# Layer 1 of a three-layer graph network: sums by one-hot products from two-half rows, and layer 2's dense pass begun inside it

## The chip, the cores and the metric

The kernel runs on one core of one Trainium2 chip. The metric is the device time of one execution in microseconds (us). The core has five engines with an instruction queue each: TensorE (PE in the profile, its weight loads PEld), VectorE (DVE), ScalarE (ACT), GpSimd (POOL) and SyncE (SP). Each runs its own queue in order and waits for the others by semaphores. The order of the instructions is written out by hand in the program.

## The reference

Three graph convolutions on 6250 nodes with 100000 edges sorted by destination, then a residual and a layer norm.

```python
src = concatenate([edge_index[0], arange(n)]); dst = concatenate([edge_index[1], arange(n)])
deg = segment_sum(ones, dst, n);  dinv = rsqrt(deg)
norm_edge = dinv[src] * dinv[dst]
h = x                                             # 6250 x 256
for W, b in ((W1, b1), (W2, b2), (W3, b3)):       # 256x512, 512x512, 512x256
    m = h @ W
    h = relu(segment_sum(m[src] * norm_edge[:, None], dst, n) + b)
return layernorm(x + h)
```

The kernel sums the rows of h before it multiplies by W where that is narrower, and scales rows by `dinv` beforehand and afterwards. Layer 1 therefore sums rows of 256 numbers, layer 2 rows of 512, layer 3 (after W3) rows of 256.

## The kernel before, in words

The nodes are split into 50 blocks of 125 (`NB`, `Q`). A layer's rows lie in a table in HBM (`tables[0..2]`, shown as `tab`), and as two halves, a rounded float32r half and what is left, in `parts` on the chip. The sum for a block is made in one of two ways.

*Dense.* The edges into a block are counted into a matrix of 125 x 6250 bytes. `counts` makes it: it compares slots of edges with running numbers (`compared`, L1043; the running numbers `runs` lie in the upper part of the PSUM bank `near_cols`), multiplies the comparisons (L1116), copies the counts to bytes (L1078) and keeps them in HBM as `kept`. Then the bytes are converted in pieces of five (`converted`, L1349) and multiplied with `parts` in 50 products of 512 columns (L1465).

*Gathered.* POOL fetches 128 rows of the table by an indirect DMA (L1381, in `gather`). In 14 rounds, row p of a gather belongs to node p of the block, and DVE adds it to the block's `total` (L1442). What lies beyond 14 edges per node comes in three gathers per block (`beyond`), one per two blocks (`pair`) and one per ten (`shared`). These rows are split into two halves by ACT and DVE (L1434, L1437) and summed by a product with a one-hot matrix (`shot`, made at L1385; product L1397).

Which rows the rounds and the gathers beyond them fetch is found by the *finder*: `found_rounds` (L589 to L621) and `found_beyond` (L630 to L668), for two blocks at a time, 17 pairs, for the blocks from 16 on. It is a generator whose steps alternate between DVE, PE and ACT. It works in the other half of the bank `near_cols` (`spot`). A part of it runs in the set-up (before the first gather), the rest one step per gather of layer 1.

`layer(i, ...)` is the loop of a layer. One turn ("chunk") is one gather. In each turn it issues a gather, sums what was gathered a few turns ago (`SPLIT`, `ADDED`), lets every unfinished block take one step of its end (`after1`, `after2`, `after3`), lets the generators in `extras` take a step, and multiplies some dense products (at most 3 per turn in layer 1).

Layer 1: 26 blocks dense (`FEW`), 24 gathered. `after1` scales a block's sum, transposes it, multiplies it by W1 (L1516), with b1 as three bf16 rows in a product of its own (L1515), and stores the row block in `tables[1]` (L1521, L78). When all dense blocks have been summed, `caching` loads `tables[1]` back into `parts`. Layer 2: 16 blocks dense in four teams of four (`teams`: 50 units a team, each of four steps of two products, L1195; 800 steps in all), 34 gathered in rounds with rows twice as wide. When the teams are done, `home` loads the new rows of layer 3 (L1222, L1223). Layer 3: 32 blocks dense, 18 gathered.

SP issues nearly all plain loads and stores in order: table rows, `kept`, the loads of `caching` and the team's counts.

Of the kernel before, what the change touches and what calls it, by code (L numbers as in the profile page):

```python
# [10 lines left out]
F32 = mybir.dt.float32  # L11
# [27 lines left out]
SPLIT_ROWS = (5, 4, 7)  # L39
# [8 lines left out]
FEW = 26  # L48
EXTRA = 0
TEAM = 4  # L50
TEAMS = 4
PACE = (8, 11)
FRONT = 12
# [7 lines left out]
SPLIT = ((3, 4, 5), (4, 5, 6), (3, 4, 6))  # L61
ADDED = (3, 5, 3)
FIRST_EDGES = TEAM * TEAMS
G = 5
GB = Q // G

WIDE = 4
RUN = 2
HOMES = 3
# [331 lines left out]
def sorted_path(ctx: ExitStack, tc: tile.TileContext, x, edges, starts, found, wts, biases, room, late, out):  # L401
# [30 lines left out]
    tables = [dram.tile([N + 1, w], F32, name=f"tab{i}") for i, w in enumerate((C, HID, C))]  # L432
    kept = dram.tile([MANY, Q, NB * Q], U8, name="kept")
# [59 lines left out]
    at_least = finder.tile([3, 2], I32, name="eatleast")  # L493
# [4 lines left out]
    nodes_since = finder.tile([P, Q], BF16, name="esince")  # L498
    row_steps = [finder.tile([P, P], BF16, name=f"esteps{n}") for n in range(2)]
# [7 lines left out]
    spot = [mat_bank[:, :256]]  # L507
    rounds_ready, beyond_ready = set(), set()

    def finder_numbers(spare):  # L510
# [11 lines left out]
        for n in range(2):  # L522
            nc.vector.tensor_single_scalar(at_least[:, n:n + 1], part[:3], float(n + 1), op=ALU.is_ge)
# [60 lines left out]
    def found_rounds(e):  # L584
# [21 lines left out]
        run = finder.tile([Q, 2, 2 * KF], F32, name="erun")  # L606
# [18 lines left out]
    def found_beyond(e):  # L625
# [25 lines left out]
        out_of = finder.tile([P, CHOSEN, WAYS], F32, name="eout")  # L651
# [4 lines left out]
        hit = finder.tile([P, CHOSEN, KF], F32, name="ehit")  # L656
        nc.vector.tensor_tensor(hit, less.unsqueeze(1).to_broadcast([P, CHOSEN, KF]),
                                place.unsqueeze(2).to_broadcast([P, CHOSEN, KF]), op=ALU.is_equal)
        value = finder.tile([P, CHOSEN, KF], F32, name="evalue")
# [12 lines left out]
    pairs_found = [e - FIRST_EDGES for e in (*range(FEW, NB, 2), *range(FIRST_EDGES, FEW, 2))]  # L672
# [80 lines left out]
    with tc.tile_pool(name="sdeg1", bufs=1) as dp1, tc.tile_pool(name="sdeg", bufs=2) as dp, \  # L753
            tc.tile_pool(name="ps_deg", bufs=2, space=bass.MemoryType.PSUM) as psd:
        ed = dp1.tile([P, NB, KF, 2], I32, name="ed")
        dlo = dp1.tile([P, NB, KF + 1], F32, name="sdlo")
# [136 lines left out]
        with tc.manual_schedule():  # L893
# [11 lines left out]
            for table in tables:  # L905
                nc.sync.dma_start(out=table[N:N + 1, :], in_=zero[:, :table.shape[1]])
# [18 lines left out]
            for k in range(NG + 2):  # L925
                for g in (k, k - 2, k - 1):
                    if 0 <= g < NG:
                        next(stages[g])
                        if k > 0:
                            search()  # L930
                        if k > FEW // GRP + 2:
                            for _ in range(3):
                                next(finding)
                g = (FEW // GRP + k - 2) * GRP
                if k >= 2 and FIRST_EDGES // GRP * GRP <= g < NB:
                    for _ in rows_risen(g, ed, find_space):
                        pass
            for g in range(FIRST_EDGES // GRP * GRP, FEW // GRP * GRP, GRP):
                for _ in rows_risen(g, ed, find_space):
                    pass  # L940
# [24 lines left out]
    hot_rooms = [room[:, 3 * MW + n * HW:][:, :HW].bitcast(BF16)[:, :WIDE * (Q + G * NB)] for n in range(HOMES)]  # L965
    first_rows = [room[:, at:at + C] for at in range(3 * MW + HOMES * HW, room.shape[1] - 4 * C - C + 1, C)]
    b1_rows = room[:3, room.shape[1] - 3 * C:][:, :C].bitcast(BF16)
# [8 lines left out]

    shots = ctx.enter_context(tc.tile_pool(name="sshots", bufs=1))
# [10 lines left out]
    pieces = one.enter_context(tc.tile_pool(name="spieces", bufs=5))  # L988
# [7 lines left out]
    totals = totals_of(one, "sfirst_totals", C, 3)  # L996
    ps_cols = ctx.enter_context(tc.tile_pool(name="sps_cols", bufs=1, space=bass.MemoryType.PSUM))
    near = ps_cols.tile([P, 512], F32, name="near_cols")
    runs_room = room[:, room.shape[1] - 4 * C:][:, :G * NB]
    nc.vector.tensor_copy(runs_room.bitcast(BF16).rearrange("p (v w) -> p v w", w=RUN), keys.unsqueeze(2).to_broadcast([P, G * NB, RUN]))  # L1000
    nc.vector.tensor_copy(near[:, :G * NB], runs_room)
    runs = near[:, :G * NB].bitcast(BF16).rearrange("p (v w) -> p v w", w=RUN)
    bias_left = work.tile([Q, HID], F32, name="szs")[:3]
    nc.sync.dma_start(out=bias_left, in_=bass.AP(tensor=b1.tensor, offset=b1.offset, ap=[[0, 3], [1, HID]]))
# [4 lines left out]
    tr_bank = ps_sum.tile([P, HID], F32, name="str")  # L1009
    common += accs + [mm_bank, tr_bank, mat_bank]  # L1010
    spot[0] = near[:, 256:]
    for n in range(3):
        whole_rows = work.tile([Q, HID], F32, name="st")[:3, :HID // 2].bitcast(BF16)
        nc.vector.tensor_copy(whole_rows, bias_left)
        nc.vector.tensor_sub(bias_left, bias_left, whole_rows)
        if n == 0:
            nc.vector.tensor_copy(b1_rows, whole_rows)
        else:
            nc.vector.copy_predicated(b1_rows, at_least[:, n - 1:n].to_broadcast([3, HID]), whole_rows)
# [4 lines left out]
    def counts(blocks, places, rush=0, at_once=False):  # L1024
# [16 lines left out]
        def compared(out, numbers):  # L1041
            shape = list(out.shape)
            nc.vector.tensor_tensor(out, runs[:, :shape[2], :shape[3]].unsqueeze(1).to_broadcast(shape),  # L1043
                                    numbers.rearrange("p (s w) -> p s w", w=shape[3]).unsqueeze(2).to_broadcast(shape),
                                    op=ALU.is_equal)
# [39 lines left out]
        for s in range(total + 4):  # L1085
            if s < total and s % WIDE == 0:
# [825 lines left out]
```

## Time and profile before

| | |
|---|---|
| median of 3 runs | 2148.16 us (2144.76 to 2149.13) |
| the profiled execution | 2138.86 us, span of its instructions 2137.0 us |
| mean granted clock of TensorE | 0.928 of full |
| PE / DVE / ACT / POOL busy | 86% / 73% / 54% / 66% of the span |
| layer 1, first to last gather | 105 to 773 us |
| layer 2, first to last gather | 826 to 1661 us |
| layer 3, from its first gather to the end | 1694 to 2137 us |

In the lines of the profile a group has line, engine, operation, output<-inputs, shapes and count, then busy us and the mean ns of one, then idle time before it and what ended that. The table by stage has a stretch, its length, the busy time of each engine with the number of instructions, the granted clock of TensorE (1 is full), the busy share of the DMA engines and GB/s. A line of waits reads: who waited, for whom, us in total, times, longest. A line of the timeline has start, length, engine, line, operation, count, and in brackets the idle time before it with what ended it. The view of one line's instructions gives shortest, median and longest ns, then the first and the last start in us.

### The profile page before, as it was taken

The numbers are of one execution on the slowest core, as the hardware profiler recorded it, in microseconds if no ns is written. First come the engines' busy times: TensorE is split into PE (matmuls) and PEld (weight loads), VectorE is DVE, ScalarE is ACT, GpSimd is POOL, SyncE is SP. The second block draws the span as 40 slices with busy tenths as digits, with TensorE's granted clock in tenths as the row PEclk, the third lists the DMA queues.
The fourth block names the chain that finished last, engine by engine and source line by source line (L and its number), as shares of the span: only waits on it lengthen the run. The fifth ranks groups of instructions, "written<-read, shape, count | busy, mean of one in ns | idle before, by whom it ended". The sixth has DMA issues, their size and how long they took to land. (4 is left out here: it accounts for less than half of the span.)

```text
span 2137.0 us, 29508 instructions
## 1 busy us (share of the span) xinstructions
PE 1839.3 (86%) x8487; PEld 1394.2 (65%) x8487; DVE 1566.4 (73%) x3295; ACT 1153.4 (54%) x2269; POOL 1407.2 (66%) x1382
## 2 busy tenths in 40 slices
PE   2448888888899995798999899899986899999995
PEld 1335655665566673576887687688764777777774
DVE  5698877887798733677777677777776378888876
ACT  0647777776688662454454344445443355555552
POOL 2075656565677733777777777777775277777775
PEclk6559999999999998899999999999997999999997
DMA  7434444444455548987777777777779377777784
GB/s 151 135 92 116 144 122 133 128 136 127 135 151 177 160 130 243 290 248 212 215 222 220 213 214 217 212 215 221 227 210 260 104 184 208 207 203 203 204 219 123
DMA packets 190147, 391.77 MB, mean 183 GB/s; under 512 B 43632, under 2 KB 106219, under 8 KB 189973
## 3 DMA queue, kind: packets, MB, share of 16 engines
q0 software_dynamic: 84816, 255.18, 42.3%
q1 hardware_dynamic: 89317, 122.76, 20.4%
q10 hardware_dynamic: 15840, 11.86, 2.2%
q8 instruction: 68, 1.11, 0.2%
q14 instruction: 106, 0.87, 0.1%
HBM read 332.63 MB, written 57.00 MB: 182 GB/s over the span
## 5 line engine op out<-in xcount | busy, mean ns | idle before, releaser
L1381 POOL DMA_INDIRECT room<-tab,round_src x1064 | 1099.2, 1033 | 529.1 <-issue 173.6
L1442 DVE TENSOR_TENSOR total<-total,room 125x256 f32<-125x256 f32 (+1 forms) x1030 | 552.0, 536 | 110.0 <-DMA room<-tab,round_src 93.1
L1349 ACT CAST piece<-room 125x625 fp32r<-125x625 uint8 x477 | 340.7, 724 | 94.8 <-PE win_ps L1465 32.7
L1381 POOL DMA_INDIRECT room<-tab,over_src x266 | 275.9, 1037 | 113.9 <-issue 42.7
L1043 DVE TENSOR_TENSOR room<-near_cols,slots 128x500 bf16<-128x500 bf16 (+1 forms) x326 | 246.5, 797 | 57.1 <-ACT epast L637 20.4
L1172 ACT CAST both<-parts 125x512 fp32r<-125x512 f32 x200 | 123.8, 619 | 278.5 <-PE smm L1195 277.9
L1465 PE MATMUL win_ps<-parts,piece 125*125 125x512 f32 x900 | 252.3, 419 | 0.8 <-ACT piece L1349 0.8
L1174 DVE TENSOR_TENSOR both<-parts,both 125x512 fp32r<-125x512 f32 x200 | 137.7, 689 | 149.1 <-ACT both L1172 148.9
L1434 ACT CAST halves<-room 128x256 fp32r<-128x256 f32 (+1 forms) x275 | 138.7, 508 | 142.3 <-DMA room<-tab,over_src 91.5
L1437 DVE TENSOR_TENSOR halves<-room,halves 128x256 fp32r<-128x256 f32 (+1 forms) x275 | 146.2, 541 | 91.2 <-ACT halves L1434 89.6
L1465 PE MATMUL smm<-parts,piece 125*125 125x512 f32 x705 | 191.7, 414 | 5.9 <-DVE piece L1349 5.8
L1465 PEld LDWEIGHTS win_ps<-parts,piece 125*125 125x125 f32 x900 | 162.1, 192 | 43.3 <-issue 8.2
L1397 PE MATMUL sacc<-halves,shot 128*125 128x512 f32 x475 | 157.0, 425 | 38.4 <-DVE halves L1437 25.9
L1465 PE MATMUL mat_ps<-parts,piece 125*125 125x512 f32 x700 | 190.1, 411 | 0.0
L1195 PE MATMUL sacc<-both,team_piece 125*125 125x512 f32 x400 | 139.9, 424 | 54.5 <-ACT team_piece L1162 20.8
L1465 PE MATMUL sacc<-parts,piece 125*125 125x512 f32 x450 | 150.5, 449 | 0.0
L1465 PEld LDWEIGHTS smm<-parts,piece 125*125 125x125 f32 x705 | 124.4, 188 | 38.1 <-DVE piece L1349 6.7
L1465 PEld LDWEIGHTS mat_ps<-parts,piece 125*125 125x125 f32 x700 | 122.5, 186 | 34.7 <-issue 8.0
L1397 PEld LDWEIGHTS sacc<-halves,shot 128*125 128x125 f32 x475 | 93.2, 198 | 76.6 <-DVE halves L1437 39.5
L1195 PE MATMUL mat_ps<-both,team_piece 125*125 125x512 f32 x400 | 137.6, 426 | 0.5 <-DVE room L1556 0.5
L1195 PE MATMUL near_cols<-both,team_piece 125*125 125x512 f32 x400 | 135.1, 420 | 0.6 <-DVE room L1556 0.5
L1195 PE MATMUL smm<-both,team_piece 125*125 125x512 f32 x400 | 134.5, 418 | 1.1 <-DVE room L1556 1.1
(417 smaller groups left out, 3243.4 us busy)
## 6 DMA issues: line engine op xcount, KB each, us to landing
kept<-room SPq DMA_DIRECT2D x32, 683.6 KB
room<-kept SPq DMA_DIRECT2D x32, 683.6 KB
room<-tab,round_src POOLq DMA_INDIRECT x1064
parts<-tab SPq DMA_DIRECT2D x35, 448.0 KB
tab<-st SPq DMA_DIRECT2D x60, 224.0 KB
room<-kept SPq DMA_DIRECT2D x160, 68.4 KB
room<-in_x SPq DMA_DIRECT2D x50, 112.0 KB
out<-st ACTq DMA_DIRECT2D x50, 112.0 KB
```

What stands on the lines that cost most here:

```text
L1043: nc.vector.tensor_tensor(out, runs[:, :shape[2], :shape[3]].unsqueeze(1).to_broadcast(shape), numbers.rearrange("p (s w) -> p s w", w=sha ...
L1172: nc.scalar.copy(to[:, :HID], row)
L1174: nc.vector.tensor_sub(to[:, HID:], row, to[:, :HID].bitcast(F32))
L1195: nc.tensor.matmul(team_banks[n][:Q], lhsT=team_pieces[u % 2][:, n, :], rhs=both_parts[u % 2][:, h * HID:(h + 1) * HID], start=(u % NB == ...
L1349: convert(piece, made_or_read[:, c * PIECE:(c + 1) * PIECE, :])
L1381: nc.gpsimd.indirect_dma_start(out=row, out_offset=None, in_=tables[i], in_offset=bass.IndirectOffsetOnAxis(ap=at, axis=0))
L1397: nc.tensor.matmul(acc[:Q, :size], lhsT=hots[b][:, k], rhs=two[:, c0:c0 + size], start=(k == c0 == 0), stop=(k == BEYOND + 1 and c0 + size ...
L1434: nc.scalar.copy(two[:, :width], landed[chunk - hi_lag])
L1437: nc.vector.tensor_sub(two[:, width:], landed.pop(chunk - lo_lag), two[:, :width].bitcast(F32))
L1442: nc.vector.tensor_add(own, parts[:, b].bitcast(F32) if i == 1 and r == 0 else own, landed.pop(chunk - ADDED[i])[:Q])
L1465: nc.tensor.matmul(acc_d[:Q], lhsT=got[done // PIECE][:, k % PIECE, :], rhs=parts[:, k], start=(k == 0), stop=(k == NB - 1))
```

## The change

Layer 1 gets a loop of its own, `first_layer`.

- 21 blocks are dense instead of 26. The count matrices of 26 are made as before (`EXTRA = 5`).
- 29 blocks are gathered. Each takes 16 gathers, straight from the sorted edges (`first_src`: 128 runs of 16 edges per block), with one gather per ten blocks for what lies beyond 2048 edges. No rounds, adds or `total` are used. Each gather is summed by a product with a one-hot matrix (`more_hots`, four at a time), that is 17 products per block.
- Blocks 21 to 25 gather plain f32 rows of 256 and multiply them as f32. Blocks 26 to 46 gather from a new table `both_halves`, whose rows hold both halves (512 numbers). It is stored from `parts` in ten stores of five blocks during the first gathers (`both_stored`). Blocks 47 to 49 gather plain rows again and split them.
- The finder needs nothing ready for layer 1: all its steps run inside layer 1, one per gather.
- The comparisons of `counts` work on five slots at a time, with f32 numbers, in two instalments, instead of on four with pairs of bf16 numbers.
- b1 is added by DVE from a copy on all partitions, instead of by a product.
- `teams` begins at the first gather of block 47, one or two steps per gather. It waits until 26 count matrices are kept, the first row is cached, the finder is done and its four banks are free. In layer 2 its steps are spread so that they end 70 gathers before the layer does (`team_goal`).

```diff
-SPLIT_ROWS = (5, 4, 7)
+SPLIT_ROWS = (7, 4, 7)
...
-FEW = 26
-EXTRA = 0
+FEW = 21
+EXTRA = 5
+BOTH_FROM = 26
+BOTH_LAG = 5
+TAIL_FROM = 47
+TAIL_LAG = 7
...
-PACE = (8, 11)
-FRONT = 12
+FRONT = 24
+TEAMS_END = 70
...
-WIDE = 4
-RUN = 2
-HOMES = 3
+WIDE = 5
...
+    both_halves = dram.tile([N + 1, 2 * C], F32, name="both")
...
-                        if k > FEW // GRP + 2:
-                            for _ in range(3):
-                                next(finding)
...
-            while FEW - FIRST_EDGES + 1 not in rounds_ready:
-                next(finding)
-                if seen == 0:
-                    next(searches)
+                if k == NG - 1:
+                    nc.vector.tensor_copy(first_src, ed[:, FEW:, :, 0])
...
-    runs = near[:, :G * NB].bitcast(BF16).rearrange("p (v w) -> p v w", w=RUN)
+    nc.vector.tensor_copy(near[:, :G * NB], keys)
+    numbered = [near[:, :G * NB]]
...
-            nc.vector.tensor_tensor(out, runs[:, :shape[2], :shape[3]].unsqueeze(1).to_broadcast(shape),
-                                    numbers.rearrange("p (s w) -> p s w", w=shape[3]).unsqueeze(2).to_broadcast(shape),
-                                    op=ALU.is_equal)
+            nc.vector.tensor_tensor(out, numbered[0][:, :shape[2]].unsqueeze(1).to_broadcast(shape),
+                                    numbers.unsqueeze(2).to_broadcast(shape), op=ALU.is_equal)
...
+                compared(hot_lo, slots[:, 0, w:w + WIDE])
+                compared(hot_key[:, :3], slots[:, 1, w:w + 3])
+            if s < total and s % WIDE == 2:
+                compared(hot[s // WIDE][1][:, 3:], slots[:, 1, w + 1:w + WIDE - 2])
...
+        while len(stored) < FEW + EXTRA or 0 not in cached or len(beyond_ready) < NE:
+            yield 1
...
+    def first_layer(gathered, dense, first, spacing, extras):
...
+        for n, b in enumerate(gathered):
+            if n == 0 or b % GRP == 0:
+                items.append((b // GRP, None, None))
+            items += [(n, b, j) for j in range(KF)]
...
+        def more_hots():
+            c0 = len(hots) * HOTS
+            n = min(HOTS, len(gathered) * (KF + 1) - c0)
+            if n > 0:
+                hot = onehot.tile([P, HOTS, Q], F32R, name="shot")
+                nc.vector.tensor_tensor(hot[:, :n], numbered[0][:, :Q].unsqueeze(1).to_broadcast([P, n, Q]),
+                                        dlo[:, FEW:].rearrange("p b j -> p (b j)")[:, c0:c0 + n].unsqueeze(2).to_broadcast([P, n, Q]),
+                                        op=ALU.is_equal)
+                hots.append(hot)
...
+            nc.gpsimd.indirect_dma_start(out=row, out_offset=None, in_=table,
+                                         in_offset=bass.IndirectOffsetOnAxis(ap=at, axis=0))
...
+                if row.dtype != F32R:
+                    hot = hot.bitcast(F32)
+                nc.tensor.matmul(acc[:Q, :row.shape[1]], lhsT=hot, rhs=row, start=(not own_product and k == 0), stop=(k == KF))
...
+                while to_sum <= chunk - lag:
+                    product(to_sum)
+                    to_sum += 1
...
+                front(chunk - tail_at)
+                until = min(len(dense) * NB, int((chunk + 1 - first) * NB / spacing), done + 3)
...
-            if k == 0:
-                nc.tensor.matmul(y_ps, lhsT=ones_p[:3, :Q], rhs=b1_rows, start=True, stop=False)
...
+        nc.vector.tensor_add(y, y_ps, b1_sb[:Q])
...
+    def both_stored(first):
+
+        for b in (*range(first, NB, GRP // 2), *range(0, first, GRP // 2)):
+            to = slice(b, b + GRP // 2)
+            by_rows(nc.sync, parts[:, to].bitcast(F32),
+                    both_halves[b * Q:(b + GRP // 2) * Q, :].rearrange("(b p) c -> p b c", p=Q), store=True)
+            yield 5
...
+    def front(since):
+        if since >= 0:
+            for _ in range(2 if since % 2 else 1):
+                next(team_work, None)
...
+    def team_goal(chunk, total):
+        most = NB * TEAM * TEAMS
+        goal = min(most, steps_before + (chunk + 1) * (most - steps_before) // (total - TEAMS_END))
+        for _ in range(3):
+            if team_steps < goal or goal == most and not teams_done:
+                next(team_work, None)
```

More of the change, by code (lines that the diff above doesn't have):

```diff
@@ L1174, in half @@
                     nc.vector.tensor_sub(to[:, HID:], row, to[:, :HID].bitcast(F32))
+        while len(stored) < FEW + EXTRA or 0 not in cached or len(beyond_ready) < NE:
+            yield 1
+        numbered[0] = cols
+        for bank in team_banks:
+            while bank is not near and not any(one is bank for one in common):
+                yield 1
+            for _ in range(len(common)):
+                one = common.popleft()
+                if one is not bank:
+                    common.append(one)
         fetch_counts(0)
         fetch_counts(1)
-        yield 1
+        yield 4
         counts_of(0)
@@ L1338, in ended @@
             most = LATE if chunk < total - 2 * KF else 1
-            going.append([chunk + late + min((3, SOON, LATE)[i], most), after(b, acc, bank, own), most])
+            going.append([chunk + late + min((None, SOON, LATE)[i], most), after(b, acc, bank, own), most])
             for item in going:
@@ L1470, in layer @@
                         ended(chunk, dense[m], acc_d, bank)
[L1471 removed]
+            assert not [item for item in fixed if item[1] is not loading]
             while going:
```

331 lines of the change are left out of this document (230 added, 101 removed).

## The prediction, made before the change was run

> **What bounds the kernel now.** I read the page, then a table by stage, the row of the finder, the waits of layer 1 and the timeline at the end of layer 1.
>
> ```profile
> span 2137.0 us, 29508 instructions
> ...
> core 0: us, PE busy (x) PEld busy (x) DVE busy (x) ACT busy (x) POOL busy (x), PEclk, DMA share, GB/s
> 105.00:580.00 475.00, 388.06 (x2056) 267.23 (x2057) 386.69 (x925) 328.48 (x687) 288.79 (x284) 0.91 0.44 126
> 580.00:772.00 192.00, 185.81 (x853) 128.17 (x852) 156.34 (x323) 151.15 (x288) 143.70 (x144) 0.99 0.54 160
> 772.00:826.00 54.00, 35.24 (x136) 23.62 (x135) 5.90 (x14) 20.16 (x36) 0.95 (x1) 0.89 0.62 171
> 826.00:900.00 74.00, 57.65 (x199) 40.92 (x200) 46.99 (x72) 32.20 (x57) 53.84 (x53) 0.80 0.95 268
> 900.00:1600.00 700.00, 656.78 (x2882) 528.08 (x2880) 511.20 (x797) 326.87 (x616) 538.59 (x515) 0.98 0.76 220
> 1600.00:1661.00 61.00, 38.77 (x164) 31.44 (x165) 40.23 (x56) 22.03 (x35) 33.36 (x33) 0.80 0.92 251
> ...
> core 0: us, POOL busy (x), PEclk, DMA share, GB/s
> 105.00:580.00 475.00, 282.20 (x279) 0.91 0.44 126
> 580.00:772.00 192.00, 142.48 (x143) 0.99 0.54 160
> ...
> L662 DVE TENSOR_REDUCE eplace<-evalue x17: 269/270/271, 135.8 to 589.4; 128x7 f32<-128x112 f32 x17
> ```
>
> The smaller table counts gathers (L1381). Layer 1 has three stretches. From 105 to 580 there are 279 gathers, 475/279 = 1.70 us each, and no engine is full: PE has 388.06/279 = 1.39 us of work per gather, DVE 1.39, POOL about 1.0. L662 is the end of a finder step for a pair; its last one starts at 589. So this slow stretch is the one in which the finder runs. From 580 to 772 a gather takes 192/143 = 1.34, PE is busy 97%, POOL 0.99 of 1.34 before its fixed gap of 0.30. From 772 to 826 nothing is gathered. Layer 2 then gathers each 700/515 = 1.36.
>
> ```profile
> POOL room L1381 <- DVE total L1442: 67.6, 69, 2.6
> ACT epast L637 <- PE near_cols L635: 48.0, 31, 5.3
> ...
> PE near_cols L635 <- DVE room L1043: 28.0, 19, 4.3
> ...
> DVE room L1043 <- ACT epast L637: 20.4, 25, 2.9
> ```
>
> These are waits between 140 and 580. A finder step passes from DVE to PE to ACT, one station per gather, in a bank (near_cols) that the comparisons (L1043) also read. The in-order engines are thereby tied to within about a gather of each other, and each burst of one is waited for by the others: 1.70 against 1.39.
>
> ```profile
> 772.06 0.95 POOL L1381 DMA_INDIRECT room<-tab,over_src  x1 [0.30 <-issue]
> ...
> 775.43 10.46 PE L1465 MATMUL str<-parts,piece 125*125 125x512 f32 x44
> ...
> 785.72 11.73 PE L1465 MATMUL win_ps<-parts,piece 125*125 125x512 f32 x50
> ...
> 801.25 0.43 PE L1515 MATMUL mat_ps<-room,eones 3*125 3x512 bf16 x1
> 801.60 1.12 PE L1516 MATMUL mat_ps<-w,room 128*125 128x512 f32 x2
> ...
> 813.85 0.69 ACT L1521 ACTIVATE st<-sacc,sdinv 125x512 f32<-125x512 f32 x1 [6.97 <-DMA tab<-st]
> ...
> 826.08 0.94 POOL L1381 DMA_INDIRECT room<-tab,round_src  x1 [53.07 <-DMA parts<-tab]
> ```
>
> The hole: two dense blocks are behind and are multiplied after the last gather, then three blocks go through the end of the layer, and layer 2's first gather needs the last stored row.
>
> **The change, part by part.** Prices:
>
> ```profile
> L1442 DVE TENSOR_TENSOR total<-total,room 125x256 f32<-125x256 f32 x588 | 247.2, 420 | 64.6 <-DMA room<-tab,round_src 54.9 <-DMA total<-tab 2.7 <-issue 0.8
> L1437 DVE TENSOR_TENSOR halves<-room,halves 128x256 fp32r<-128x256 f32 x152 | 62.3, 420 | 46.9 <-ACT halves L1434 46.4 <-issue 0.2
> L1043 DVE TENSOR_TENSOR room<-near_cols,slots 128x1000 bf16<-128x1000 bf16 x162 | 192.0, 1185 | 0.0
> L1043 DVE TENSOR_TENSOR room<-near_cols,slots 128x500 bf16<-128x500 bf16 x163 | 67.7, 415 | 57.1 <-ACT epast L637 20.4 <-PE near_cols L635 11.4 <-ACT egot L602 7.7
> L1385 DVE TENSOR_TENSOR shot<-scols,over_lo 128x625 fp32r<-128x625 f32 x76 | 61.2, 805 | 0.0
> L1549 DVE SCALAR_TENSOR_TENSOR szs<-sacc,sdinv,total 125x512 f32<-125x512 f32 x34 | 25.3, 745 | 4.0 <-PE sacc L1397 4.0
> L613 DVE TENSOR_TENSOR w_sb<-erun,ebegin 125x448 f32<-125x448 f32 x17 | 10.7, 627 | 0.6
> ...
> 1656.67 1.89 PE L1615 MATMUL str<-w,room 128*125 128x256 f32 x8
> ```
>
> *Gathers.* Before, 24 blocks of 14 + 3 gathers and 15 shared make 423. After, 29 x 16 + 3 = 467. *PE.* A 512-wide product costs 10.46/44 = 0.24 us. An f32 product 256 wide leaves two records (L1615: 8 for 4 products), so 1.89/4 = 0.47. Per gather the change takes away 120/423 = 0.28 products (0.07 us) and the bias product (0.35 between its start and the next one's, at 0.12 blocks per gather: 0.04). It adds 17/16 = 1.06 products: 0.50 us in the first 85 gathers, whose rows are plain f32, 0.25 later. Net +0.39 and +0.14: PE has 1.78, later 1.53 per gather. The 250 dense products fewer shorten the dense part, not its rate (at most 3 per gather).
>
> *DVE.* Away: 0.79 adds and 0.2 halvings of 0.42: -0.42. The comparisons for four slots cost 1.60 us, 0.40 a slot. With an f32 source I price them at the slope of the slow rows, (1185 - 805)/375 = 1.01 ns per element: 0.81 + 0.93 + 0.68 = 2.42 for five slots, 0.48 a slot; at 1.5 slots per gather +0.12. One-hots: four for 0.68, +0.18. The bias add at 0.745: +0.09. Sum -0.03: DVE stays at 1.36. The exchange that looks like a gain for DVE is paid back by slower comparisons, one-hots and bias.
>
> [...]
>
> *The finder* takes 17 pairs x 17 steps = 289 gathers at one step each, now all inside layer 1. *First stretch:* cost between PE's load at 97% (1.84 and 1.58) and the whole addition on top of 1.70 (2.09 and 1.84). The idle 0.31 of PE can swallow most of 0.14, not 0.39; I take 1.88 and 1.75, near the lower end: 85 x 1.88 + 204 x 1.75 = 517 (478 to 553). *Second stretch,* dense without finder: 350 gathers of dense work + 16 - 289 = 77; PE 1.30 + 0.14 at 97% = 1.48: 114 (POOL alone: 103; at 1.6: 123). *Third,* 101 gathers without dense work, beside the loading of 50 blocks: the nearest row is layer 2's first stretch with the same loads, 74/53 = 1.40, for the 53 gathers of double rows, 1.34 for the rest: 138 (135 to 150). Here the teams' first steps, some 72 of 800, run under POOL's cover. Without that cover they would cost 72 x 2 x 0.24 = 35.
>
> *Start:* two pairs' steps leave the set-up (two of the 0.63 products, two sums as long, small ones): -4 (-10 to 0). *SP* gets 100 stores of both halves, 12.8 MB, in the first 60 gathers, ahead of rows and counts; at 0.44 of DMA I cost them at nothing; if they delayed the double gathers until they end, +10. *Hole:* dense work ends 100 gathers earlier, so the last block is left alone: landing, split, product, the four steps to the row and its store: 20 (12 to 45) for 54.
>
> Layer 1 to the next first gather: 101 + 517 + 114 + 138 + 20 = 890 for 826, +64. Layer 2 keeps its 603 gathers and POOL's 1.36, so 72 steps fewer for PE bring nothing in the middle. Its end (61 us for 33 gathers, 16 too many) loses the teams but keeps the loads that follow them: -5 (-18 to +3). Layer 3's comparisons are off the path: 0 (to +6). Sum: 2137 + 59 = 2196 span, 2138.86 + 59 = 2198 for that execution. The median of the runs lies 9.3 us above it: 2207.
>
> **The rivals.** *The ties fall away (faster).* Without adds, POOL no longer waits for DVE (67.6 us of the waits shown), and PE runs the first stretch at 97%: 478, -39; the hole shrinks to 12, -8; the loads at 1.34, -3; layer 2's end -18 rather than -5, -13. That gives 2207 - 63 = 2144. For it: 580 to 772 shows PE at 97%. Against it: there is no finder there, and the finder stays. It comes out level when the first stretch falls to 458 us, 1.58 per gather, other terms kept.
>
> [...]
>
> *DVE becomes the tie (slower still).* Comparisons, in two instalments now, and one-hots all read near_cols, which the finder writes. If each instalment waits as L1043 does, the first stretch takes 2.0 per gather: 578, 2268. It decides from DVE busy above 85% there, or from one-hots waiting for ACT.
>
> *The teams do not start early*, because counts, rows or banks are late: their 72 steps go into layer 2, 0.134 steps x 0.48 per gather, PE 1.34 of 1.36: +10, 2217.
>
> **How the numbers follow.** Forecast 0.58; ties fall 0.19, of which 0.14 ends faster by over 0.2% (about what a measurement of this kernel can tell from no change) and 0.05 within; DVE tie 0.18; late teams 0.05. Slower 0.81. Range: down to 2125, where all lower ends come together (-39 first stretch, -11 second, -3 third, -6 start, -8 hole, -13 end of layer 2: 2127); up to 2270, which takes in the DVE tie and the forecast's own upper ends (+36, +9, +12: 2264).
>
> **What would show it.** Right: about 1.8 us per gather while L662's line runs, PE above 85%, DVE about 75 to 80%; 460 or more products of one-hots near 0.24 us; no dense product after the last gather; a hole near 20 us; layer 2 at 1.36. Wrong: a first stretch below 1.6, or layer 2 below 1.30 per gather.

## The result, and the profile after

The changed kernel takes 2236.01 us (median of 4 runs, 2232.29 to 2239.73), the kernel before 2146.46 beside it: ratio 1.0424, 95% interval 1.039 to 1.0458, slower. The forecast was 2207, with a range to 2270. The profiled execution took 2235.24, its span 2233.4.

The table by stage of the changed kernel, columns as before:

```profile
102.00:265.00 163.00, 126.87 (x666) 94.33 (x667) 118.36 (x236) 88.46 (x172) 84.31 (x82) 0.94 0.57 173
265.00:655.00 390.00, 332.32 (x1791) 234.96 (x1791) 270.80 (x580) 240.38 (x488) 203.90 (x215) 0.98 0.71 185
655.00:773.00 118.00, 113.37 (x530) 81.60 (x528) 90.67 (x148) 85.17 (x152) 80.47 (x86) 1.00 0.93 246
773.00:852.00 79.00, 52.57 (x153) 28.74 (x153) 47.75 (x73) 31.78 (x55) 43.45 (x47) 0.67 1.21 300
852.00:870.00 18.00, 9.44 (x15) 3.85 (x15) 6.13 (x13) 4.67 (x11) 11.90 (x13) 0.59 0.96 254
870.00:879.00 9.00, 1.95 (x4) 1.31 (x5) 1.96 (x5) 3.09 (x7) 0.71 (x2) 0.50 0.58 145
879.00:923.00 44.00, 42.07 (x165) 30.03 (x164) 30.11 (x64) 28.44 (x67) 33.82 (x33) 0.98 0.59 168
```

The same for the gathers of layer 1 alone (now L1365), for its two stretches beside the finder and the one after it.

```profile
102.00:265.00 163.00, 83.07 (x81) 0.94 0.57 173
265.00:655.00 390.00, 198.98 (x211) 0.98 0.71 185
655.00:773.00 118.00, 79.24 (x85) 1.00 0.93 246
```

And the end of the finder's steps in the view of one tile, and from the timeline the last dense products of layer 1, the last gather of layer 1 and the first of layer 2:

```profile
L662 DVE TENSOR_REDUCE eplace<-room x17: 269/270/272, 153.1 to 651.9; 128x7 f32<-128x112 f32 x17
...
770.93 0.71 PE L1450 MATMUL str<-parts,dense_rows 125*125 125x512 f32 x2
...
921.63 0.94 POOL L1365 DMA_INDIRECT room<-tab,efirst_src  x1 [0.30 <-issue]
...
939.36 0.95 POOL L1561 DMA_INDIRECT room<-tab,round_src  x1 [16.78 <-DMA parts<-st]
```

While the finder runs, to 652 us, a gather takes 163/81 = 2.01 and then 390/211 = 1.85 us, 1.89 on average, against 1.70 before. PE is busy 83% of it (459.2 of 553 us) and DVE 70%, so no engine is full there. PE has 459.2/292 = 1.57 us of work per gather, where it had 1.39 before. After it, 655 to 773, a gather takes 1.39 with PE at 96%. No dense product is left after the last gather. From 773 to 852, where the loads of `caching` meet the double rows, the DMA engines are at their fullest (share 1.21, 300 GB/s) and TensorE is granted 0.67.

Laid against the steps of the prediction:

| | before | predicted | measured |
|---|---|---|---|
| first gather | 105 | 101 | 102.7 |
| beside the finder | | 517 | 552.3 (to 655) |
| dense, no finder | | 114 | 118 |
| beside the loads | | 138 | 149.6 |
| hole | 54 | 20 | 16.8 |
| layer 2's first gather at | 826.1 | 890 | 939.4 |
| from there to the end of the span | 1310.9 | 1306 | 1294.0 |

The span grew by 96.4: 113.3 more up to layer 2, 16.9 less behind it. The 517 us beside the finder were forecast for 289 gathers; the 552.3 hold 292. The question for the experiments is why that stretch takes 552 us.

### The profile page after: what moved, and what is told of

It reads as the page before. It is cut to its first block, busy times and chain, and to the rows that moved or that the text cites. A ratio compares the mean times of both kernels' runs of the same rounds, so it can differ in the third digit from the quotient of the medians.

```text
span 2233.4 us, 29538 instructions
## 1 busy us (share of the span) xinstructions
PE 1887.6 (85%) x8654; PEld 1433.4 (64%) x8654; DVE 1583.6 (71%) x3141; ACT 1121.3 (50%) x2183; POOL 1434.9 (64%) x1426
## 5 line engine op out<-in xcount | busy, mean ns | idle before, releaser
L1561 POOL DMA_INDIRECT room<-tab,round_src x728 | 765.8, 1052 | 265.9 <-issue 132.8
L1621 DVE TENSOR_TENSOR total<-total,room 125x512 f32<-125x512 f32 (+1 forms) x694 | 410.6, 592 | 82.8 <-DMA room<-tab,round_src 72.0
L1365 POOL DMA_INDIRECT halves<-both,efirst_src x318 | 300.5, 945 | 240.7 <-PE sacc L1399 59.6
L1032 DVE TENSOR_TENSOR room<-near_cols,slots 128x625 bf16<-128x625 f32 (+2 forms) x390 | 300.2, 806 | 119.8 <-PE near_cols L638 31.9
L1164 DVE TENSOR_TENSOR dense_rows<-parts,dense_rows 125x512 fp32r<-125x512 f32 x200 | 137.9, 689 | 133.8 <-ACT dense_rows L1162 131.5
L1271 ACT CAST piece<-room 125x625 fp32r<-125x625 uint8 x217 | 151.8, 713 | 106.3 <-PE win_ps L1644 35.1
L1365 POOL DMA_INDIRECT room<-tab,efirst_src x128 | 128.4, 1003 | 102.6 <-PE smm L1399 31.0
L1195 PE MATMUL sacc<-dense_rows 125*125 125x512 f32 x400 | 140.9, 427 | 43.1 <-DVE dense_rows L1164 16.8
L1271 ACT CAST dense_rows<-room 125x625 fp32r<-125x625 uint8 x210 | 149.3, 724 | 6.6 <-PE smm L1450 1.9
L1195 PE MATMUL mat_ps<-dense_rows 125*125 125x512 f32 x400 | 136.4, 423 | 0.5 <-DVE room L1740 0.5
L1195 PE MATMUL smm<-dense_rows 125*125 125x512 f32 x400 | 135.2, 419 | 1.1 <-DVE room L1740 1.1
L1321 DVE TENSOR_TENSOR shot<-near_cols,edlo 128x500 fp32r<-128x500 f32 x110 | 74.0, 673 | 77.5 <-PE sacc L1399 29.4
```

The costliest lines, as they stand in the source:

```text
L1032: nc.vector.tensor_tensor(out, numbered[0][:, :shape[2]].unsqueeze(1).to_broadcast(shape), numbers.unsqueeze(2).to_broadcast(shape), op=AL ...
L1164: nc.vector.tensor_sub(to[:, HID:], row, to[:, :HID].bitcast(F32))
L1195: nc.tensor.matmul(team_banks[n][:Q], lhsT=team_pieces[u % 2][:, n, :], rhs=both_parts[u % 2][:, h * HID:(h + 1) * HID], start=(u % NB == ...
L1271: convert(piece, matrix[:, c * PIECE:(c + 1) * PIECE, :])
L1365: nc.gpsimd.indirect_dma_start(out=row, out_offset=None, in_=table, in_offset=bass.IndirectOffsetOnAxis(ap=at, axis=0))
L1561: nc.gpsimd.indirect_dma_start(out=row, out_offset=None, in_=tables[i], in_offset=bass.IndirectOffsetOnAxis(ap=at, axis=0))
```

## The experiments

**Theory.** The comparisons (L1032) and the one-hots (L1321) read the running numbers from `near_cols`, the bank in which the finder works with PE and ACT. If the in-order engines are tied to one another there, the PE work that the change adds cannot use PE's idle time. The waits of the changed kernel between 265 and 655 (who, for whom, us in total, times, longest) speak for it:

```profile
POOL halves L1365 <- PE sacc L1399: 47.9, 42, 4.9
ACT epast L640 <- DVE shot L1321: 31.5, 14, 5.2
ACT epast L640 <- DVE room L1032: 31.2, 16, 3.6
...
DVE room L1032 <- PE near_cols L638: 26.3, 21, 4.2
...
DVE room L1032 <- ACT epast L640: 19.3, 20, 4.2
...
PE near_cols L638 <- DVE room L1032: 15.3, 11, 2.6
```

**Rivals.** PE's added work alone sets the pace, or the loads and the teams' early steps do. The experiments ran on three chips, each set of them on one. On two of these the kernel before takes 2449 and 2455 us, so times and ratios are compared within a set. Where the length of a stretch is set beside one from another chip, the text says so. The chips are told apart by the time of the kernel before: the first is that of the result above (2146), the second takes 2455, the third 2143, the fourth 2449. Whether the first is one of the others is not on record.

**All numbers in SBUF.** In the changed kernel:

```diff
-    nc.vector.tensor_copy(near[:, :G * NB], keys)
-    numbered = [near[:, :G * NB]]
+    numbered = [keys]
```

> The changed kernel, with the running numbers of the comparisons and one-hots in a bf16 tile on the chip instead of in the bank near_cols, in which the finder works. Theory (the shared bank ties the engines): the waits between DVE L1032/L1321 and ACT L640 or PE L638 go (they sum to some 200 us between 102 and 655), and the stretch with the finder, 552 us for 293 gathers (1.89 each) in the changed kernel, falls to 1.70 or less, about 500 us; the total falls by 40 to 60 us, to about 2185. Rival (PE's own load and the finder's chain of steps set the pace, wherever the numbers lie): the stretch stays within 1.85 to 1.93 per gather and the total within 10 us of 2236. Rival (DVE now takes both inputs from the chip's memory and POOL suffers for it): gathers above 1.05 us each on POOL and no gain.

Measured 2422.32 us against 2455.21 of before, on the second chip: 0.9848 (0.9812 to 0.9883), faster than before there. It ran again on the fourth, together with three others:

> The changed kernel with all running numbers in SBUF once more, beside the three others of this set. The chip of its first run took some 14% longer for every kernel, in layers 2 and 3 above all, so its ratio of 0.985 is not one to set against 1.042. If the shared bank costs the first stretch some 80 us on any chip: ratio 1.00 to 1.01 where the kernel before takes 2145, and 0.985 again where it takes 2455. If the layers 2 and 3 of this kernel are also better off than those of before: below 0.995 on either.

Measured 2419.5 against 2448.67, 0.9888 (0.9845 to 0.9931). What this kernel's ratio is on a chip that takes 2145 us for the kernel before was not measured. An estimate: its finder ends 59 us earlier than that of the changed kernel on the third chip (594 against 653, below); if all of it arrived there, 2228.85 - 59 = 2170 us, 1.012 of the kernel before. So these two ratios below 1 do not show that the change pays on such a chip. The table by stage of the second run, all engines and then its gathers alone, the finder's row, and the costliest shape of comparison and of one-hot:

```profile
265.00:590.00 325.00, 303.61 (x1680) 217.19 (x1679) 253.88 (x559) 225.18 (x459) 225.77 (x203) 0.99 0.79 208
...
265.00:590.00 325.00, 220.40 (x199) 0.99 0.79 208
...
L662 DVE TENSOR_REDUCE eplace<-room x17: 269/270/271, 148.1 to 593.9; 128x7 f32<-128x112 f32 x17
...
L1031 DVE TENSOR_TENSOR room<-keys,slots 128x750 bf16<-128x750 bf16 x130 | 121.6, 935 | 0.0
...
L1320 DVE TENSOR_TENSOR shot<-keys,edlo 128x500 fp32r<-128x500 bf16 x110 | 74.4, 677 | 101.2 <-PE sacc L1398 19.1 <-PE smm L1398 15.2 <-issue 11.2
```

And the same shapes in the changed kernel:

```profile
L1032 DVE TENSOR_TENSOR room<-near_cols,slots 128x750 bf16<-128x750 f32 x130 | 121.0, 931 | 0.0
...
L1321 DVE TENSOR_TENSOR shot<-near_cols,edlo 128x500 fp32r<-128x500 f32 x110 | 74.0, 673 | 77.5 <-PE sacc L1399 29.4 <-PE smm L1399 11.7 <-PE near_cols L638 10.0
```

The instructions last about as long (935 and 931, 677 and 673 ns), the work is the same, only the place of the numbers differs (and their type, f32 in the bank and bf16 in SBUF). Yet PE goes from 85% to 93% busy and a gather from 1.85 to 325/199 = 1.63 (and from 102 to 265 us from 2.01 to 163/89 = 1.83). The waits of the finder's ACT for comparisons and one-hots (31.5 and 31.2 us) are gone. The finder ends at 594 in both runs. In the changed kernel it ended at 652 on the first chip, and on the second, the chip of the first of these two runs, at 673 and 675 in two variants that differ from the changed kernel only behind that point (below). So the shared bank costs the first stretch 80 us on one chip and some 60 across chips, and without it the pace comes near the 1.84 and 1.58 that the prediction priced for PE at 97%.

In the changed kernel the numbers lie in other columns of the bank (the first 250) than the finder's work (from 256 on), and the engines wait for each other all the same: between 265 and 655 ACT's sign waits 31.5 us for one-hots and 31.2 for comparisons, and the comparisons wait 26.3 for PE and 19.3 for ACT. What happens in one bank without such waits no run here shows.

**One tie or the other.** The one-hots alone, then the comparisons alone, read from SBUF:

```diff
-                nc.vector.tensor_tensor(hot[:, :n], numbered[0][:, :Q]...
+                nc.vector.tensor_tensor(hot[:, :n], keys[:, :Q]...
```
```diff
-            nc.vector.tensor_tensor(out, numbered[0][:, :shape[2]]...
+            nc.vector.tensor_tensor(out, keys[:, :shape[2]]...
```

> The changed kernel with the one-hots alone made from numbers in SBUF; the comparisons still read the shared bank. If the one-hots are what the change ties to the finder (110 of them, on every fourth product), most of the 80 us that numbers in SBUF took from the first stretch come back here: last L662 near 610, against 673 with all in the bank and 594 with none. If the comparisons in two instalments are, only 15 to 25 us come back: last L662 near 650. If each tie alone suffices to hold the engines together, less than 10: above 663.

> The changed kernel with the comparisons alone fed from SBUF; the one-hots still read the finder's bank. One-hots alone from SBUF took 18 us from the finder's stretch (last L662 at 635 against 653), all numbers about 75. If the comparisons' tie carries the rest, last L662 is near 595 and the ratio 1.01 to 1.02; if either tie by itself holds the engines together, last L662 is above 625 and the ratio above 1.03. POOL's gathers, 0.95 us each with numbers in the bank and 1.15 with all in SBUF, should be near 1.1 here if the reads of SBUF by DVE stretch them.

The changed kernel as it is ran in the first one's set, on the third chip, and not on the second as its expectation has it:

> The changed kernel as it is, on the chip on which the kernels with loads half as often and without early teams ran, so that those can be set against it. Either theory expects it slower than the kernel before; the two experiments beside which it is to be laid gave ratios of 1.014 and 1.018, so 1.01 to 1.045. First stretch (last L662) near 673 us if the chips differ in layers 2 and 3 alone, as their first stretches say.

It took 2228.85 against 2143.26: 1.0417 (1.0389 to 1.0446), the first result again, its finder ending at 653. One-hots alone: 2214.16, 1.0347 (1.0319 to 1.0376); the finder ends at 635, 18 us earlier, as expected if the comparisons carry most of the tie (15 to 25). Comparisons alone, on the fourth chip: 2431.39, 0.994 (0.9914 to 0.9966), where all numbers in SBUF gave 0.9888 in the same set; the finder ends at 611.8 against 593.9, again 18 us apart, between the two cases expected. Its ratios had been expected too high, for a chip like the first. The finder's rows of the changed kernel (third chip), of one-hots alone and of comparisons alone:

```profile
L662 DVE TENSOR_REDUCE eplace<-room x17: 269/270/270, 152.3 to 653.0; 128x7 f32<-128x112 f32 x17
...
L662 DVE TENSOR_REDUCE eplace<-room x17: 269/270/272, 151.8 to 635.1; 128x7 f32<-128x112 f32 x17
...
L662 DVE TENSOR_REDUCE eplace<-room x17: 269/270/273, 147.5 to 611.8; 128x7 f32<-128x112 f32 x17
```

So, as far as ends from two chips can be set beside each other, the two ties add up: the one-hots are worth 18 us whether or not the comparisons are freed, and the comparisons carry the other 40 to 60. Neither by itself keeps up the whole tie.

**The finder ahead of the gathers,** in the changed kernel and in the kernel before:

```diff
         with tc.manual_schedule():
+            for _ in finding:
+                pass
```

> The changed kernel, with all steps of the finder run at once ahead of layer 1's first gather. Theory (the finder's steps cost the pace, not the load): after the first gather, the stretch with dense work runs at 1.45 to 1.5 per gather, as 655 to 773 does in the changed kernel (118 us for 85), so some 378 gathers take about 560 us instead of 670; ahead of it stand 100 to 250 us of finder alone, so the total is 2236 to 2370. Rival (PE's products and dense work alone set the pace): the stretch stays at 1.75 or more per gather.

> The kernel before with the finder run to its end ahead of the first gather, so that nothing of it lies beside gathers. In the changed kernel the finder alone took 155 us, and gathers beside dense work then took 1.53 us each. Here the finder should take 135 to 155 alone, and a gather then 1.34 to 1.40 (as in the second stretch of before, PE at 97%): so the finder costs the kernel before 279 x (1.70 - 1.37) = 92 us beside the gathers, against (1.89 - 1.53) x 293 = 105 in the changed kernel. If the first stretch was slow for another reason than the finder, gathers stay at 1.6 or more in the first 280.

Measured, one run each: 2546.77 against 2455.21 (second chip), and 2189.53 against 2143.26 (third chip). In the kernel before, the finder alone and the gathers after it (all engines, then gathers alone):

```profile
120.00:272.00 152.00, 56.60 (x536) 36.90 (x536) 60.35 (x245) 54.67 (x158) 0.00 (x0) 1.00 0.00 1
300.00:700.00 400.00, 387.27 (x1756) 269.68 (x1755) 346.97 (x740) 319.99 (x600) 305.61 (x308) 1.00 0.56 165
...
300.00:700.00 400.00, 298.12 (x302) 1.00 0.56 165
```

In the changed kernel, with the gathers alone split into those of plain f32 rows (to 403 us) and, in the last row, those of double rows:

```profile
122.00:279.00 157.00, 57.30 (x540) 37.79 (x541) 65.32 (x254) 57.48 (x161) 0.00 (x0) 1.00 0.04 12
...
420.00:800.00 380.00, 352.53 (x1597) 254.23 (x1595) 265.31 (x466) 243.80 (x429) 239.39 (x253) 0.98 0.84 224
...
283.00:403.00 120.00, 69.33 (x73) 0.97 0.59 181
...
420.00:800.00 380.00, 233.25 (x248) 0.98 0.84 224
```

The finder is a chain of steps from engine to engine: 152 and 157 us alone, with no engine above 42%. Free of it, a gather takes 400/302 = 1.32 in the kernel before (PE 97%), just below the 1.34 to 1.40 expected. In the changed one it takes 120/73 = 1.64 with plain f32 rows and 380/248 = 1.53 with double rows (PE 93%), a little above the 1.45 to 1.5 expected and below the rival's 1.75. (The total of 2236 to 2370 was expected for a chip that takes 2146 us before.) Beside the gathers the finder thus costs about 284 x (1.70 - 1.32) = 108 us in the kernel before, and about 81 x (2.01 - 1.64) + 211 x (1.85 - 1.53) = 97 in the changed one (its 1.64 and 1.53 are from another chip than the 2.01 and 1.85, as is the 1.32 than the 1.70). So the finder costs no more after the change than before it. What the change adds beside it, 0.31 us per gather early and 0.15 later over the 1.70, is nearly the PE work that the prediction priced, 0.39 and 0.14, so nearly all of that work comes on top.

**The kernel before with its numbers in SBUF:**

```diff
-    nc.vector.tensor_copy(near[:, :G * NB], runs_room)
-    runs = near[:, :G * NB].bitcast(BF16).rearrange("p (v w) -> p v w", w=RUN)
+    runs_tile = one.enter_context(tc.tile_pool(name="srunsb", bufs=1)).tile([P, G * NB], F32, name="runs_sb")
+    nc.vector.tensor_copy(runs_tile, runs_room)
+    runs = runs_tile.bitcast(BF16).rearrange("p (v w) -> p v w", w=RUN)
```

> The kernel before with its running numbers (bf16 pairs) in SBUF and no longer in the finder's bank. Theory of the shared bank: the tie costs the kernel before as well, where DVE waited 20.4 us for ACT's sign and 11.4 for PE, and the finder's ACT and PE waited for the comparisons (28.0 PE for DVE): the first stretch goes from 1.70 us per gather toward 1.55, 279 x 0.15 = 40 us less, ratio 0.975 to 0.99; the 500-element comparison stays at 415 ns. Rival (the bank costs much only where one-hots read it too): 10 us less at most, ratio 0.995 to 1.0.

Measured 2130.17 against 2143.26, 0.9948 (0.993 to 0.9966): faster, but only 13 of the 40 us: in total the rival's case, though not by its mechanism, as the finder did end 37 us earlier (552.4, against 589.4 in the kernel before on the first chip). Why the rest did not arrive is in POOL's groups, first before (140 to 580, first chip), then here (140 to 550; the row of L1044 is of the whole run):

```profile
L1381 POOL DMA_INDIRECT room<-tab,round_src x209 | 205.3, 982 | 134.6 <-DVE total L1442 40.1 <-issue 33.3 <-DVE halves L1437 11.7
```
```profile
L1382 POOL DMA_INDIRECT room<-tab,round_src x209 | 244.7, 1171 | 66.8 <-issue 24.1 <-DVE total L1443 15.6 <-DVE room L1044 9.4
...
L1044 DVE TENSOR_TENSOR room<-runs_sb,slots 128x500 bf16<-128x500 bf16 x163 | 67.2, 412 | 2.4 <-PE mat_ps L1117 2.4
...
550.00:640.00 90.00, 69.92 (x58) 0.94 0.46 134
```

The comparisons' own waits are gone (2.4 us idle before L1044, where 57.1 stood before L1043). But a gather now keeps POOL busy for 1.17 us instead of 0.98, and this goes on when the finder has ended: from 550 to 640 (the last row, gathers alone) POOL works 69.92/58 = 1.21 per gather and a gather takes 90/58 = 1.55, where the kernel before took 1.34. With the fixed gap of 0.30 after each gather (0.30 to 0.31 before each one from 690 to 727), 1.21 makes 1.51 of the 1.55: here POOL sets the pace. The changed kernel's gathers last longer in the same way: 0.946 us with the numbers in the bank, 0.974 with the one-hots' alone in SBUF, 1.065 with the comparisons' alone, 1.108 with all. The rows, in this order (from 265 us to about where the finder ends):

```profile
L1365 POOL DMA_INDIRECT halves<-both,efirst_src x203 | 192.1, 946 | 174.2 <-PE sacc L1399 47.9 <-PE win_ps L1399 27.7 <-PE str L1399 25.0
...
L1365 POOL DMA_INDIRECT halves<-both,efirst_src x197 | 191.9, 974 | 155.2 <-PE sacc L1399 43.2 <-PE win_ps L1399 26.8 <-issue 17.9
...
L1365 POOL DMA_INDIRECT halves<-both,efirst_src x192 | 204.6, 1065 | 119.7 <-issue 30.8 <-PE sacc L1399 26.0 <-PE str L1399 12.2
...
L1364 POOL DMA_INDIRECT halves<-both,efirst_src x191 | 211.6, 1108 | 95.6 <-issue 35.4 <-PE sacc L1398 11.9 <-PE win_ps L1398 9.9
```

So with all numbers in SBUF a gather lasts 0.16 us longer in the changed kernel (1.108 for 0.946) and 0.19 in the kernel before (1.171 for 0.982), each pair from two chips; what holds it up the traces do not show. Numbers in the bank spare POOL (0.946 us a gather in the changed kernel) and tie the finder (its end at 652); numbers in SBUF do the reverse (1.108, and 594).

**Three lesser questions.** The first five gathered blocks split into halves too, on top of all numbers in SBUF:

```diff
-            return 0 <= c < total and items[c][1] is not None and items[c][1] >= TAIL_FROM
+            return 0 <= c < total and items[c][1] is not None and not BOTH_FROM <= items[c][1] < TAIL_FROM
```

> As the kernel above, with the gathers of the first five gathered blocks split into halves by ACT and DVE too, so that each has one product of 512 at 0.24 instead of an f32 one of 256 at 0.47. With numbers in SBUF PE is busy 93% of the first stretch, so if PE sets the pace there: 80 x 0.23 = 18 us less, ratio 0.008 below the kernel above. Rival: DVE, at 85% from 102 to 190 us, gets 80 x 0.42 = 34 us more and becomes the bound, so nothing or a few us more.

Measured 2452.59, 1.0012 (0.9987 to 1.0038), 33 us above the kernel without this edit in the same set: slower, by more than the few us of the rival, and not by DVE's load. DVE is as busy from 102 to 190 as without it (71.2 and 72.1 us); POOL waits for the rows that the splitting holds (from 102 to 265):

```profile
POOL room L1364 <- DVE halves L1419: 34.3, 23, 4.4
```

So, with the numbers in SBUF, f32 products at twice PE's price (0.47 us against 0.24, from the rows of L1615 and L1465 of the kernel before) were the better choice there.

The loads of `caching` at half the rate (`yield 3` to `yield 6`), and no early steps of the teams (`front` and the loop at layer 1's end issue none):

> The changed kernel, with the loads of layer 1's rows back onto the chip one per 7 gathers instead of one per 4. Theory (from 773 to 852 the loads and the double-width gathers together fill the DMA engines: 47 gathers at 1.68, DMA share 1.21): the stretch after the dense work falls to about 1.4 per gather, 95 gathers from 150 to about 133 us; what is not loaded by the end of layer 1 is loaded in layer 2's first 80 gathers, which lose 5 to 10 us; total 5 to 12 us below the changed kernel. Rival (the same bytes only move): total within 5 us, the slow stretch moves into layer 2. Rival (the stretch is slow because of counts and the start of the teams, not DMA): 1.55 or more per gather as now.

> The changed kernel, with the teams begun in layer 2 only (no step of them in layer 1; their end 70 gathers before the layer's end is kept). Theory (layer 2 is bound by POOL at 1.36 per gather, the early steps buy nearly nothing): total within 12 us of the changed kernel, the hole at the end of layer 1 shorter or equal (18 us), and the 9 us stop of the gathers at 870 gone; layer 2 still about 1.36 to 1.38 per gather. Rival (early steps are what shortens the way from layer 2's first gather to the end, 1294 us after against 1311 before): that way grows by 15 us or more.

Measured 2491.34, 1.0143 (1.0095 to 1.0192), and 2498.73, 1.018 (1.0158 to 1.0201), where the numbers in SBUF gave 0.985 in the same set. Both edits act only behind the finder's stretch, whose end they leave at 673 and 675, so neither rival explains the 552 us. With half the loads, the 93 gathers from the last dense product on take 152/93 = 1.63 us each (802 to 954), as in the changed kernel on the first chip (151.6/93), and not 1.4: that theory missed. Without the early steps the stop of POOL at the teams' start is gone, as expected (no gather from 878 to 908 us has more than 2.26 us of idle time before it, where the stop was 8.29), and the way from layer 2's first gather to the end is 1522 us in the profiled execution, against 1513 with half the loads and 1521 with the numbers in SBUF on the same chip. That is less than the rival's 15, but the executions of this one kernel lie 12 us apart (2488 to 2501), so it settles little. What each edit is worth in total stays open, as the changed kernel itself did not run on this chip.

**A fourth dense product per gather,** in the kernel before with its numbers in SBUF:

```diff
-                    until = min(until, done + 3)
+                    until = min(until, done + 4)
```

> The kernel before with numbers in SBUF and up to four dense products per gather in layer 1 instead of three. About 94 dense products come after the last gather there (10.4 + 11.7 us). If the limit of three alone holds them back, they move beside gathers and the hole falls from 51 to about 30 us: ratio near 0.985. If the dense work is held back by late count matrices, or PE has no room beside the gathers, the time moves from the hole into the gathers: 0.992 to 0.998, as without it (0.995).

Measured 2416.76, 0.9875 (0.9831 to 0.9919), near the 0.985 of the first case. No dense product is left after the last gather, and the hole is half as long as the 50.7 that the kernel without this edit had on the third chip:

```profile
886.37 0.94 POOL L1382 DMA_INDIRECT room<-tab,round_src  x1 [24.23 <-DMA room<-kept]
```

Most of what the change takes from the hole (54 to 17) can thus be had by one number. What that number is worth in time is not shown: the kernel without it ran on the third chip only, and here the finder ends at 641.6, 89 us later than there, whether for the fourth product or for the chip. This version and the changed kernel with its numbers in SBUF both beat the kernel before in the same set, on the fourth chip (0.9875 and 0.9888, whose intervals overlap).

## Why the prediction was right, and where it was off

The sign held, and so did the mechanism that was given for it: the finder and its ties stay, and the added PE work is dearer than the shorter hole. 2236 lies in the range, 29 above the forecast. The span is 37 above (2233.4 for 2196); the forecast had put the median of the runs 9.3 us above the profiled execution, and it lies 0.8 above, so the 29 is 8 smaller than the 37 by luck. The terms fail as follows.

- *First stretch, the mis-sized term:* 517 predicted, 552 measured. The step that failed is "the idle 0.31 of PE can swallow most of 0.14, not 0.39; I take 1.88 and 1.75, near the lower end". Almost nothing was swallowed: of the 2.01 and 1.85 measured, the first is 0.08 below and the second 0.01 above the bounds with the whole addition on top (2.09 and 1.84). The prediction had named the ties and then let PE's idle time be used in spite of them. With the numbers in SBUF it is used (1.83 and 1.63).
- *PE and DVE per gather:* DVE priced at 1.36, measured (118.36 + 270.80)/292 = 1.33; the comparisons at 0.81, 0.93 and 0.68 us, measured 0.810, 0.931 and 0.676 (the first and last from their groups, counted over the run). PE over the first stretch is 459.2/292 = 1.57, where 1.78 and 1.53 weigh to 1.60. The work was priced right; the overlap was not. For the same reason two of the prediction's own signs of being right did not come: PE is at 83% beside the finder, not above 85, and DVE at 70%, not at 75 to 80, as the same work is spread over more time.
- *Second stretch:* 118 for 114, 85 gathers instead of 77, at 1.39 and not 1.48.
- *Third stretch:* 149.6 for 138. The double rows beside the loads took 79/47 = 1.68, not 1.40: the row taken from layer 2 had DMA at 0.95, here it is 1.21. That the full DMA is the cause is argued, not shown: half the loads did not shorten the stretch as a whole. And POOL stood still for 8.29 us when the teams began (without their early steps it did not):

```profile
878.80 1.01 POOL L1365 DMA_INDIRECT room<-tab,efirst_src  x1 [8.29 <-ACT dense_rows L1152]
```

- *Hole:* 16.8 for 20, right. *Start:* 102.7 for 101. (The range's upper end leaves out what the prediction itself allowed for the hole, up to 45, and for SP's stores, +10; neither came.)
- *Layer 2 and after:* 16.9 less where 5 was forecast, near the lower end of -18. This error of 12 in the other direction hides a third of the first stretch's 35. Layer 2 gathers from 939 to 1763, 11 us less than before, and the hole to layer 3 (23.2 for 32.8) is 10 shorter; layer 3 is 3 longer. *SP's stores* at nothing: right, the last was issued at 203.5 us, and the first double gather went out at 265.1.
- *Rivals.* "The ties fall away" needed 1.58 per gather to come out level; only the moved numbers came near it. "DVE becomes the tie" had the mechanism that is in the waits, ACT's sign waiting for one-hots and comparisons in the bank (31.5 and 31.2 us), but its test, DVE above 85%, was the wrong one: DVE is at 70%, and the tie here needed no busy engine. Its price, 578, was 26 too high, nearer to the 552 than the forecast's 517. "Teams do not start early" fails: their first product is at 877.

## What to carry to other kernels

When engines are tied to one another by a shared bank, do not count the idle share of an engine in that stretch as room: price work added to any of them as coming fully on top (here 0.31 and 0.15 us per gather were added where 0.39 and 0.14 of work had been priced), until a run with the tie removed shows otherwise. Ask of each constant that an engine reads over and over where it lies: in a PSUM bank in which others work it tied the engines here (the finder's end came 80 us later on the second chip), in SBUF it went with longer gathers on POOL (1.108 us for 0.946), and which was dearer depended on what ran beside it (from 550 to 640 the kernel before took 1.55 us per gather with its numbers in SBUF, and 1.34 after its finder with them in the bank, on another chip). And a stretch in which a chain of small steps runs (150 us alone, no engine above 42%) is worth the experiment that moves it aside, as that shows at once what it costs its neighbours. Compare kernels on one chip only: here the kernel before took 14% longer on two chips (2449 and 2455 us) than in the other two sets of runs (2143 and 2146).

## What was not expected of the hardware

- Two chips took 2449 and 2455 us for the kernel before where the other two sets of runs took 2143 and 2146. The changed kernel with half the loads or without early teams came to layer 2's first gather at 977 and 965 us on such a chip, against 939 in the first profile, but to its end at 2490 and 2487 against 2233: most of the difference lies in layers 2 and 3. There, from 1000 to 1700, a gather takes 700/429 = 1.63 us in the changed kernel with its numbers in SBUF (second chip), and 700/512 = 1.37 in the changed kernel (third chip), though the two kernels differ only in the place of layer 1's numbers. In the traces of the second and fourth chips ACT and DVE stand still for several us at a time, and the profile names no instruction of this core that released them ("remote"); the traces of the first and third show no such wait. ACT's longest waits in layer 2 (1000 to 1600), second chip, then third:

```profile
ACT dense_rows L1161 <- PE smm L1194: 161.8, 60, 8.3
ACT dense_rows L1161 <- remote: 75.0, 15, 10.9
```
```profile
ACT dense_rows L1162 <- PE smm L1195: 221.9, 115, 6.2
ACT halves L1613 <- DMA room<-tab,over_src: 41.1, 22, 6.5
```

What holds the engines up on those chips was not settled.
- An indirect gather costs POOL 0.946 to 0.98 us beside comparisons out of PSUM, and 1.11 to 1.17 beside the same comparisons and one-hots out of SBUF.
- The 500-element bf16 comparison takes 412 ns out of SBUF and 415 out of PSUM: the place of that operand made no difference to this instruction here.
